# A 7 x 7 softmax-weighted convolution on one core: other slots of taps, 32-row tiles for the two small layers, logits computed twice

## The chip, the core and the metric

One core of one Trainium2 chip runs the whole program in one launch. The metric is the device time in microseconds (us) of that launch. Five engines work side by side, each through its own list in order, and wait for one another through semaphores: TensorE (PE, with its weight loads as PEld), VectorE (DVE), ScalarE (ACT), GpSimd (POOL) and SyncE (SP), which issues most DMAs.

## What is computed

The program has two layers. The second (attention and a feed-forward part on chosen tokens) is not touched and follows the first. The first is, on 4 images of 256 channels and 56 x 56 pixels, after a group normalization:

```
x1 = conv1x1(x, w1, b1)            # 32 channels
x2 = conv1x1(x, w2, b2)            # 32 channels
x3 = conv1x1(x, w3, b3)            # 256 channels
p  = conv1x1(position(h, w), wp, bp)   # 2 channels, the same for all images
sub2 = x1[:, :, None] - unfold_patches(x2)     # 49 taps, reflected borders
subp = p[:, :, None] - unfold_patches(p)
y = relu(bn_eval(concatenate([sub2, subp]), bn1))   # 34 channels
y = relu(bn_eval(conv1x1(y, cw1), bn2))             # 32 channels
wgt = softmax(conv1x1(y, cw2, cb2), axis=taps)      # 32 channels x 49 taps
out[:, l, s] = sum over taps of x3[tap][:, l, s] * wgt[:, l, tap]   # s: 8 channels share a weight
x = x + out
```

All is float32.

## The kernel before

`conv_layer` first makes *planes*: image by image, in strips of 8 rows (`planes(n, q)`, 7 strips an image), it normalizes x, makes x1, x2 and x3 and stores them in DRAM, x2 and x3 with their reflected borders (`x3d`), x1 in `a1d`. Strips of later images are made while earlier images are worked on.

The main work goes in *blocks* of 4 rows, 14 an image, 56 in all. The 49 taps of a block are packed into *slots*: one instruction on 128 partitions handles four taps (four groups of 32 channels), because a group reads its plane one column or one row further on. Here there are 13 slots (`SLOTS`), 10 with four taps and 3 with three (96 partitions). For column slots the planes sit in rings (`xc` for x3, `ac` for x2), for row slots in windows loaded anew for each block (`xw`, `aw`).

A block passes through three generators:

- `relation`: `differ` (POOL, x1 - x2 in four groups of slots), `bend` (ACT, relu), `hidden` (PE, layer cw1 with a block-diagonal 128 x 128 matrix, by pairs of slots), `bend_more` (ACT, slot by slot, since in the inside of the image the position term is one number per slot, held in `tb`), the six border columns apart (`borders`, `place_borders`, `bend_borders`), `logits` (PE, layer cw2), `keep` (ACT, to SBUF in `lg`).
- `softmax`: `begin`, `largest`, `split`, `join`, `turned`, `over_turned` (the maximum over slots and over the four groups, by a tree on DVE and two turns on PE), `lower` (DVE, subtract it), `exponents` (ACT), `add_up`, `gather`, `spread`, `invert` (the sum's reciprocal).
- `values`: for each slot a product of 8 planes with the slot's exponentials, 128 x 1792 elements, 8 slots on DVE (`OURS`, the weights copied to PSUM first by `weights`) and 5 on POOL (`POOLS`), and `add`, four matmuls with the matrix `same` that add the groups up in PSUM (`acc`); then `divide`, `more` (+ x) and `store`.

`by_quarters` splits a 128-column layer into four matmuls with 32 columns, which lie in four column parts of the array (the profile's "128*32": 128 rows, 32 columns). The trace shows two matmul records for each float32 matmul.

The order is written out by hand: `AT` gives for each step of a block its place in a round, in steps of a fourteenth of a round (`ROUND = 14`) and a rank. The loop at the end of `conv_layer` emits one round per block, with steps of three or four blocks mixed. `InOrder` keeps that order on each engine. `side` holds the planes, the statistics of the next image, and `ready`, the second layer's normalization of image 0, which advance one piece per step. SP issues the loads in the same order (`load_relation`, `load_first`, `load_values`).

Of the kernel before, what the change touches and what calls it, by code (L numbers as in the profile page):

```python
# [15 lines left out]
P = 128  # L16
NB = 4
# [41 lines left out]
def bn_affine(nc, pool, par, n, eps, tag):  # L59
# [15 lines left out]
    [(ki, 0, COLUMN, 4) for ki in range(KS)]  # L75
    + [(0, kj, ROW, 4) for kj in range(4, KS)]
    + [(ki, 4, COLUMN, 3) for ki in range(4, KS)]
)
NS = len(SLOTS)
ORDER = [0, 1, 2, 3, 4, 5, 6, 10, 11, 12, 7, 8, 9]  # L80
POOLS = [1, 3, 5, 7, 9]
OURS = [i for i in range(NS) if i not in POOLS]
GROUPS = [(0, 4), (4, 7), (7, 10), (10, 13)]
HALVES = [(0, 10), (10, 13)]
INNER = W - 2 * PAD
RB = 4
ROUND = 14
KEPT = 12
RING = KEPT + 3
QUADS = (H + 2 * PAD + 3) // 4  # L90
FB4 = RB * W


AT = {
    "load_relation": (-12, 4), "load_first": (23, 4), "load_values": (32, 5), "differ": (-5, 6),
    "bend": (-2, 9), "load_pos": (-1, 7), "hidden": (4, 5), "borders_0": (1, 5),
    "place_borders_0": (3, 9), "bend_borders_0": (6, 9), "borders_1": (3, 5),
    "place_borders_1": (7, 0), "bend_borders_1": (14, 3), "bend_more": (5, 5), "logits": (7, 1),
    "keep": (8, 7), "begin": (22, 1), "largest_0": (23, 3), "largest_1": (25, 6), "split": (27, 0),
    "join": (27, 7), "turned_0": (28, 7), "over_0": (29, 1), "turned_1": (29, 4), "over_1": (30, 1),  # L100
    "lower_0": (30, 1), "exp_0": (31, 0), "lower_1": (32, 5), "exp_1": (32, 8), "lower_2": (31, 9),
    "exp_2": (33, 0), "add_up_0": (33, 4), "add_up_1": (33, 5), "gather": (34, 1),
    "spread": (34, 1), "invert": (36, 1), "weights": (31, 5), "ours": (33, 0), "add_ours": (34, 0),
    "pools": (33, 6), "add_pools": (36, 9), "divide": (47, 1), "more": (51, 7), "store": (55, 3),
}
PLANE = WP * WP
NPL = SH + 1
# [3 lines left out]
def conv_layer(ctx: ExitStack, tc: tile.TileContext, d, xs: bass.AP, ln0: bass.AP):  # L111

# [7 lines left out]
    a1d = dram.tile([NB, REL, HW], F32, name="a1d")  # L126
    posd = dram.tile([8, NS, 3 * FB4], F32, name="posd")
    bordersd = dram.tile([8, NS, 3 * FB4], F32, name="bordersd")
    insided = dram.tile([8, NS], F32, name="insided")

# [6 lines left out]
    chunk = lambda q: slice(q * CH, (q + 1) * CH)  # L137

# [4 lines left out]
    for q in range(NCH):  # L143
        sy.dma_start(x0[:, :, chunk(q)], whole_image(x, 0)[:, :, chunk(q)])

    par = const.tile([P, len(COLS)], F32, name="par")
    nc.scalar.dma_start(par, d["par"])
    pposs = const.tile([8 * NS, 7], F32, name="pposs")
    nc.scalar.dma_start(pposs, d["par_pos"])
    gavg = const.tile([P, P], F32, name="gavg")  # L150
    nc.scalar.dma_start(gavg, d["gavg"])
    w12 = const.tile([P, 2, 2 * REL], F32, name="w12")
    nc.scalar.dma_start(w12, d["w12T"].rearrange("(c p) o -> p c o", p=P))
    w3 = const.tile([P, 2, C], F32, name="w3")
    nc.scalar.dma_start(w3, d["w3T"].rearrange("(c p) o -> p c o", p=P))
    cw1 = const.tile([P, P], F32, name="cw1")
    nc.scalar.dma_start(cw1, d["cw1_diag"])
    cw1p = const.tile([8, P], F32, name="cw1p")
    nc.scalar.dma_start(cw1p, d["cw1_pos"])
    cw2 = const.tile([P, P], F32, name="cw2")  # L160
    nc.scalar.dma_start(cw2, d["cw2_diag"])
    turn = const.tile([P, 2, P], F32, name="turn")
    nc.scalar.dma_start(turn, d["turn"])
    same = const.tile([P, P], F32, name="same")
    nc.scalar.dma_start(same, d["same"])
    eps = const.tile([P, 1], F32, name="eps")
    nc.vector.memset(eps, GN_EPS)

# [5 lines left out]


    sh12 = const.tile([P, 1], F32, name="sh12")
    nc.vector.tensor_scalar(sh12[:REL], s1[:REL], col("b1")[:REL], t1[:REL], ALU.mult, ALU.add)
    nc.vector.tensor_scalar(
        sh12[REL : 2 * REL], s1[REL : 2 * REL], col("b2")[REL : 2 * REL], None, ALU.mult
    )  # L180

    mm = ctx.enter_context(tc.tile_pool(name="mm", bufs=4, space=PSUM))
    xqp = ctx.enter_context(tc.tile_pool(name="xq", bufs=3))
# [3 lines left out]
    held = {}  # L187

    def load(n, q):

        t = xqp.tile([P, 2, CH], F32, tag="xq", name=f"xq{n}_{q}")
        sy.dma_start(t, whole_image(x, n)[:, :, chunk(q)])
        return t

    def statistics(n):

        st = sp.tile([P, 2, NCH, 6], F32, tag="st", name=f"st{n}")
        mv = sp.tile([P, 2, 2], F32, tag="mv", name=f"mv{n}")
        ts = held.pop(("xa", n))
        for q in range(NCH):  # L200
            for c in range(2):
                ve.bn_stats(st[:, c, q], ts[q][:, c])
            if len(ts) < NCH:
                ts.append(load(n, len(ts)))
            yield
        yield
        for c in range(2):
            ve.bn_aggr(mv[:, c], st[:, c].rearrange("p q s -> p (q s)"))
        pm = mm.tile([P, 512], F32, tag="mm", name=f"pm{n}")
        te.matmul(pm[:, 0:2], gavg, mv[:, :, 0], start=True, stop=True)  # L210
        yield
        gm = sp.tile([P, 2], F32, tag="gm", name=f"gm{n}")
        ve.tensor_copy(gm, pm[:, 0:2])
# [4 lines left out]
        pv = mm.tile([P, 512], F32, tag="mm", name=f"pv{n}")  # L218
        te.matmul(pv[:, 0:2], gavg, dv, start=True, stop=True)
        rs = sp.tile([P, 2], F32, tag="rs", name=f"rs{n}")  # L220
        se.activation(rs, pv[:, 0:2], AF.Sqrt, bias=eps)
# [10 lines left out]
    held["xa", 0] = [x0[:, :, chunk(q)] for q in range(NCH)]  # L232

    tb = const.tile([P, NS], F32, name="tb")
    near = const.tile([P, 3, NS * RB * 2 * PAD], F32, name="near")
# [5 lines left out]
    for j in range(2):  # L244
        nc.scalar.dma_start(loc[j * 4 * NS : (j + 1) * 4 * NS, :, 1], d["loc_from"])
    whole(statistics(0))

    def positions():

        pl = pp.tile([8 * NS, 2, 3 * FB4], F32, name="pl")  # L250
        ve.tensor_scalar(pl, loc[:, 0], pposs[:, 4:5], None, ALU.mult)
        yield
        ve.scalar_tensor_tensor(pl, loc[:, 1], pposs[:, 5:6], pl, ALU.mult, ALU.add)
        yield
        ve.tensor_scalar(pl, pl, pposs[:, 6:7], None, ALU.add)
        cen = pp.tile([8 * NS, 3 * FB4], F32, name="cen")
        ve.tensor_tensor(cen, pl[:, 0], pl[:, 1], ALU.subtract)
        yield
        se.activation(cen, cen, AF.Relu, bias=tp1, scale=sp1)
        inside = pp.tile([8 * NS, 1], F32, name="inside")  # L260
        ve.tensor_copy(inside, cen[:, FB4 + W // 2 : FB4 + W // 2 + 1])
        less = pp.tile([8 * NS, 3 * FB4], F32, name="less")
        ve.tensor_scalar(less, cen, inside, None, ALU.subtract)
        for j in range(2):
            r = slice(j * 4 * NS, (j + 1) * 4 * NS)
            nc.sync.dma_start(insided.rearrange("(g j) t -> j t g", j=2)[j], inside[r])
            nc.scalar.dma_start(bordersd.rearrange("(g j) t f -> j t g f", j=2)[j], cen[r])
            nc.sync.dma_start(posd.rearrange("(g j) t f -> j t g f", j=2)[j], less[r])
        at8 = pp.tile([8, NS], F32, name="at8")
        nc.sync.dma_start(at8, insided)  # L270
        edge = pp.tile([8, 3, NS, RB, 2, PAD], F32, name="edge")
        for b in range(3):
            for i in range(2):
                at = b * FB4 + i * (W - PAD)
                src = bordersd[:, :, at : at + 1]
                nc.scalar.dma_start(
                    edge[:, b, :, :, i],
                    bass.AP(
                        src.tensor, src.offset,
                        [list(src.ap[0]), list(src.ap[1]), [W, RB], [1, PAD]],  # L280
                    ),
                )
        for _ in range(10):
            yield
        pt = mm.tile([P, 512], F32, tag="mm", name="pinside")
        te.matmul(pt[:, :NS], cw1p, at8, start=True, stop=True)
        ve.tensor_scalar(tb, pt[:, :NS], s2, t2, ALU.mult, ALU.add)
        n = NS * RB * 2 * PAD
        for b in range(3):
            pt = mm.tile([P, 512], F32, tag="mm", name=f"pnear{b}")  # L290
            te.matmul(
                pt[:, :n], cw1p, edge[:, b].rearrange("p t h i w -> p (t h i w)"),
                start=True, stop=True,
            )
            ve.tensor_scalar(near[:, b], pt[:, :n], s2, t2, ALU.mult, ALU.add)

    second = slice(REL, 2 * REL)

    def planes(n, q):


        sh, rs = held["norm", n]
        f = slice(q * CH, (q + 1) * CH)
        at = f"{n}_{q}"
        t = held.pop(("xb", n, q))
        for c in range(2):
# [4 lines left out]
        issue = [sy, se] if n == 0 and q < 2 else [sy]  # L311
        yield
        pt = mm.tile([P, 512], F32, tag="mm", name=f"p12_{at}")
        for c in range(2):
            quartered(pt[: 2 * REL, :CH], w12[:, c], t[:, c], start=c == 0, stop=c == 1)
        yield
# [1499 lines left out]
```

## Time and profile before

| | us |
|---|---|
| median of 3 runs (lowest, highest) | 3694.44 (3693.19, 3697.65) |
| the profiled execution, and its span from first to last instruction | 3699.99, 3698.2 |
| span: until the first block's `divide` | 169.1 |
| first to last `divide` of the 56 blocks (55 steps) | 1631.6 |
| after the last `divide`: the second layer | 1897.5 |

The busy time of each engine between the first and the last `divide` is PE 1464.9, DVE 1497.2, ACT 1146.3, POOL 1412.3 of 1631.6 us; the DMA engines are busy 63% of it and move 135 GB/s. By image, taken from `divide` to `divide`:

| stretch of the span, us | length | PE | DVE | ACT | POOL | DMA |
|---|---|---|---|---|---|---|
| 169.1 to 581.4 | 412.3 | 376.3 | 376.9 | 304.5 | 340.6 | 65% |
| 581.4 to 1009.7 | 428.3 | 388.5 | 394.4 | 309.9 | 367.9 | 66% |
| 1009.7 to 1433.0 | 423.3 | 380.4 | 377.8 | 298.7 | 361.8 | 63% |
| 1433.0 to 1800.7 | 367.7 | 319.7 | 348.3 | 233.2 | 342.1 | 57% |

A `divide` is the DVE instruction `o<-acc,rz`; the time between two of them is the time of one block. Busy time of PE holds the pipelined ends of its matmuls, so a stream of n matmuls is best read from start to start. In a row of the groups, "out<-in" names the tiles (numbers left out) and the shape is partitions x elements.

### The profile page before, as it was taken

The page shows a single profiled execution, that of the slowest core. Times are in us where ns is not written, and L with a number is a line of the kernel's source. Part 1 is how long each engine was busy: PE and PEld are TensorE (multiplying, and loading weights), DVE is VectorE, ACT ScalarE, POOL GpSimd, SP SyncE. Part 2 cuts the span into 40 slices and gives each one's busy share as a digit, 9 for nine tenths or more (in the row PEclk, how much of TensorE's full clock was granted, in tenths as well). Part 3 has the DMA queues.
Part 4 walks back from the last instruction along what each step waited for, and adds up shares of the span by engine and source line. Part 5 has one row for each costly group of instructions (what it writes and reads, how often), then busy time and mean ns, then how long its engine had stood idle before and what let it go on. Part 6 is the DMA issues. An engine that isn't in the chain of part 4 may idle for free. (4 is left out here: it accounts for less than half of the span.)

```text
span 3698.2 us, 92932 instructions
## 1 busy us (share of the span) xinstructions
PE 3267.4 (88%) x38326; PEld 1431.4 (39%) x38326; DVE 2559.0 (69%) x3552; ACT 1941.0 (52%) x4104; POOL 1950.9 (53%) x1165
## 2 busy tenths in 40 slices
PE   3889997999879998899699979997899889989989
PEld 1334432443334333343243334333433344336666
DVE  2589989999889988999774567555864576534211
ACT  2768766787568766776235533453344424542111
POOL 1578887889778988998650035022602252211311
PEclk7999999999989999999899999999999999999999
DMA  3766657665666647655301210132013200231110
GB/s 101 159 149 149 148 134 164 150 139 109 153 146 150 129 97 147 124 120 109 102 2 45 65 49 7 37 96 61 8 32 80 62 18 13 64 93 47 55 49 26
DMA packets 328070, 332.00 MB, mean 90 GB/s; under 512 B 68651, under 2 KB 315407, under 8 KB 327647
## 3 DMA queue, kind: packets, MB, share of 16 engines
q1 hardware_dynamic: 309509, 289.68, 35.3%
q0 software_dynamic: 11408, 32.32, 2.7%
q8 instruction: 302, 4.95, 0.6%
q10 hardware_dynamic: 6730, 4.05, 0.5%
q14 instruction: 121, 0.99, 0.1%
HBM read 256.78 MB, written 68.68 MB: 88 GB/s over the span
## 5 line engine op out<-in xcount | busy, mean ns | idle before, releaser
L859 POOL TENSOR_TENSOR pr<-xc,lg 128x1792 f32<-128x1792 f32 x280 | 1039.4, 3726 | 220.1 <-DMA xc<-x3d 92.8
L859 PE MATMUL acc<-pr,same 128*32 128x448 f32 (+1 forms) x5824 | 718.5, 554 | 126.2 <-DVE pr L859 81.0
L859 PE MATMUL p<-y,cw 128*32 128x400 f32 (+5 forms) x6272 | 679.3, 511 | 3.0 <-ACT y L859 1.8
L859 ACT ACTIVATE ph<-pg,unit 128x896 f32<-128x896 f32 x448 | 426.7, 1004 | 474.7 <-PE pg L859 471.9
L859 DVE TENSOR_TENSOR pr<-xc,exp 128x1792 f32<-128x1792 f32 x280 | 559.6, 1999 | 41.0 <-DMA xc<-x3d 29.4
L859 POOL TENSOR_TENSOR phi<-ls 128x512 f32<-128x512 f32 (+1 forms) x200 | 246.2, 1231 | 348.3 <-PE accs L859 172.8
L859 ACT ACTIVATE y<-p,tb,bn2s 128x200 f32<-128x200 f32 (+1 forms) x728 | 341.7, 521 | 144.8 <-PE p L859 143.2
L859 PEld LDWEIGHTS acc<-pr,same 128*32 128x32 f32 (+1 forms) x5824 | 203.5, 111 | 432.4 <-DVE pr L859 181.5
L859 DVE TENSOR_TENSOR phi<-pv,ls 128x1408 f32<-128x1408 f32 (+1 forms) x200 | 322.0, 1619 | 64.7 <-PE accs L859 44.0
L859 PEld LDWEIGHTS p<-y,cw 128*32 128x32 f32 (+1 forms) x6272 | 236.2, 111 | 326.4 <-issue 216.3
L859 DVE TENSOR_TENSOR pr<-xw,exp 128x1792 f32<-128x1792 f32 x168 | 338.0, 2013 | 26.8 <-DMA xw<-x3d 14.5
L859 POOL TENSOR_TENSOR y<-a,ac 128x896 f32<-128x896 f32 x168 | 279.3, 1663 | 115.7 <-DMA ac<-x3d 87.2
L859 POOL DMA_DIRECT2D out<-tk x28 | 20.9, 747 | 543.0 <-ACT tk L859 532.3
L859 ACT ACTIVATE ls<-pv 128x256 f32<-128x256 f32 (+1 forms) x200 | 77.4, 387 | 389.5 <-PE pv L859 369.1
L859 PE MATMUL pg<-qT,pairs 32*128 32x448 f32 x1792 | 275.7, 593 | 6.2 <-ACT ph L859 4.1
L859 PE MATMUL pv<-wqkv,xn 128*32 128x256 f32 x3136 | 216.1, 391 | 49.0 <-DVE phi L859 29.7
L859 POOL DMA_INDIRECT us<-rows,to x112 | 109.6, 979 | 262.5 <-DMA us<-rows,to 231.8
L859 PE MATMUL accs<-phi,v 128*32 128x512 f32 (+1 forms) x1600 | 217.7, 608 | 26.3 <-DVE phi L859 25.7
L859 ACT ACTIVATE lg<-p,par 128x448 f32<-128x448 f32 x392 | 232.8, 594 | 2.5 <-PE p L859 2.4
L859 ACT ACTIVATE y<-y 128x896 f32<-128x896 f32 x224 | 180.7, 807 | 87.1 <-POOL y L859 87.0
L859 ACT ACTIVATE h<-ph,apar 128x512 f32<-128x512 f32 (+1 forms) x104 | 63.2, 658 | 293.3 <-PE ph L859 293.2
L859 PE MATMUL acc<-ph,cf 128*32 128x448 f32 (+1 forms) x1792 | 215.0, 551 | 0.0
(256 smaller groups left out, 5168.5 us busy)
## 6 DMA issues: line engine op xcount, KB each, us to landing
xw<-x3d SPq DMA_DIRECT2D x224, 248.0 KB
xq<-in_x SPq DMA_DIRECT2D x47, 448.0 KB
xc<-x3d SPq DMA_DIRECT2D x54, 248.0 KB
xc<-x3d SPq DMA_DIRECT2D x54, 247.0 KB
xc<-x3d SPq DMA_DIRECT2D x54, 246.0 KB
xc<-x3d SPq DMA_DIRECT2D x54, 245.0 KB
xr<-in_x SPq DMA_DIRECT2D x224, 56.0 KB
xs<-xr SPq DMA_DIRECT2D x224, 56.0 KB
```

The source lines that it names most:

```text
L859: return lambda *a, **k: self.tc.keep_in_program_order(of(*a, **k))
```

## The change

Everything is inside `conv_layer` and the arrays that the host lays out for it.

**Slots.** 12 slots of four taps, 48 taps round the centre; the centre tap is handled apart with the 4 rows of a block on the four groups of partitions (56 elements instead of 224; steps named `..._own`). Every slot has 128 partitions.

```diff
 SLOTS = (
-    [(ki, 0, COLUMN, 4) for ki in range(KS)]
-    + [(0, kj, ROW, 4) for kj in range(4, KS)]
-    + [(ki, 4, COLUMN, 3) for ki in range(4, KS)]
+    [(ki, 0, COLUMN) for ki in range(3)]
+    + [(ki, 3, COLUMN) for ki in range(4, KS)]
+    + [(0, kj, ROW) for kj in range(4, KS)]
+    + [(3, kj, ROW) for kj in range(3)]
 )
+PARTS = ((0, 8), (8, 12))
+POOLS = (2, 5, 8, 11)
+OURS = tuple(t for t in range(NS) if t not in POOLS)
```

**Layers on sixteen parts.** `hidden` and `logits` multiply 32 x 32 weights, with a row part r and a column part j for each matmul, into bank r of a PSUM tile `quad` of four banks, for 8 slots and then for 4. The position term becomes a second matmul of two rows for every block (`posm`, or `posb` in border blocks); the border steps and `tb`, `near` go. `bend_more` is one ACT instruction for 8 slots and one for 4.

```diff
+            for r in range(4):
+                for j in range(4):
+                    te.matmul(
+                        quad[group(j), r, : m * FB4], cw1[group(r)],
+                        view(y1[group(r)], (a + j) * FB4, [[4 * FB4, m], [1, FB4]]),
+                        start=True, stop=False, skip_group_check=True,
+                    )
+            for r in range(4):
+                two = slice(r * REL, r * REL + 2)
...
+                    te.matmul(
+                        quad[group(j), r, : m * FB4], cw1p[two], of,
+                        start=False, stop=True, skip_group_check=True,
+                    )
```

**Logits twice.** `logits` writes them to `quad` only for the maximum: one `tensor_reduce` on DVE over 8 slots (128 x 1792 in, 128 x 56 out) and one over 4. `keep`, `begin`, `split`, `join`, `turned`, `over_turned` and `lower` go. `lowered` makes the logits again in `quad` and takes the maximum off with further matmuls by `minus`; `exponents` reads `quad` and writes the weights `ws`.

```diff
+            ve.tensor_reduce(
+                held["mm", k][:, i], view(quad, 0, [[1, W], [512, 4], [W, 4 * m]]), AX.XY, ALU.max
+            )
...
+        def lowered(i):
...
+                    te.matmul(
+                        quad[group(j), r, : m * FB4], cw2[group(r)],
+                        view(y2[i][group(r)], j * m * FB4, [[1, m * FB4]]),
+                        start=True, stop=False, skip_group_check=True,
+                    )
...
+                    te.matmul(
+                        quad[group(j), r, : m * FB4], minus[group(r)],
+                        view(mxs[group(r)], 0, [[0, m], [1, FB4]]),
+                        start=False, stop=True, skip_group_check=True,
+                    )
```

`add_up` sums over slots into 128 x 56 (52 matmuls of 56 columns), `invert` takes 56 elements, and `spread` (16 matmuls of 56 columns and 128 rows) lays the maximum, the reciprocal and the centre's weight out over 224 elements.

**PSUM.** One tile `quad` (4 banks), one bank `small` for all small results, the planes, the statistics and `ready` (`bank()`), one bank `acc`, two for `exps`; each exists once.

**Loads.** `xw` becomes a ring of rows like `xc` (`rows_kept(..., ROW)`; one new quad of 4 rows a block, and 3 rows copied behind the ring's end each third block). New per block: `x3c` (the centre of x3), `aq` (centre of x1 and x2 by rows), 7 rows instead of 4 in `aw`. x1 is stored in `x3d` with borders; `a1d` goes. Position terms are stored once in `posd`, and the small loads of 12 bytes (`edge`) go.

**Planes.** A strip is made in named steps: x1 and x2 of both halves in one PSUM tile and one ACT instruction, x3 copied by ACT instead of DVE; a strip every second block, all the way.

**Places.** A new table `AT`, with `ROUND = 250`; all steps of all blocks, planes and side pieces are sorted by place and emitted in that order.

```diff
+    "load_relation": -120, "load_places": -94, "load_planes": -48, "differ_2": 0, "differ_3": 50,
...
+    "hidden_1": 116, "bend_0": 121, "bend_more_1": 126, "edges_both": 128,
+    "store_both": 136, "load_first": 148, "hidden_0": 151, "differ_own": 170, "bend_more_0": 173,
+    "bend_own": 200, "logits_0": 209, "load_second": 235, "hidden_own": 239, "bend_more_own": 244,
+    "largest_0": 246, "logits_own": 253, "logits_1": 259, "keep_own": 263, "largest_1": 272,
+    "values_0": 273, "most": 285, "keep_values_0": 285, "spread_most": 290, "load_own": 294,
+    "keep_most": 316, "lowered_0": 322, "values_1": 326, "lower_own": 337, "exp_0": 341,
...
+    "exp_own": 363, "exp_1": 364, "weights_1": 364, "product_1": 376, "edges_values": 376,
+    "product_2": 378, "store_values": 384, "weights_3": 385, "weights_4": 389, "add_up": 394,
...
+    "divide": 603, "more": 635, "store": 647,
...
+    for _, _, name, do, of in sorted(events, key=lambda e: e[:2]):
```

## The prediction

> **What bounds it now.** I read the busy time in windows first, with the block as unit (from one `divide` to the next). The blocks come in three kinds: a plain one of 25.7 us (most of image 3), one with a strip of planes 28.8, one with planes and `ready` 33.9. Four plain blocks, one with planes, one with both; columns are length, then PE, PEld, DVE, ACT, POOL, clock, DMA share, GB/s:
>
> ```profile
> core 0: us, PE busy (x) PEld busy (x) DVE busy (x) ACT busy (x) POOL busy (x), PEclk, DMA share, GB/s
> 1490.00:1592.90 102.90, 92.86 (x1128) 42.25 (x1124) 102.14 (x97) 75.03 (x160) 102.90 (x41) 1.00 0.59 120
> ...
> 1083.00:1112.00 29.00, 27.71 (x330) 12.83 (x328) 27.08 (x27) 23.07 (x56) 26.66 (x11) 1.00 0.69 157
> ...
> 641.00:675.00 34.00, 31.85 (x370) 14.35 (x362) 31.12 (x33) 27.46 (x65) 28.72 (x12) 1.00 0.70 156
> ```
>
> In plain blocks POOL never rests (102.90 of 102.90) and DVE hardly (102.14): POOL sets the end. With planes POOL has gaps and PE has none. The groups give the durations:
>
> ```profile
> L859 POOL TENSOR_TENSOR pr<-xc,lg 128x1792 f32<-128x1792 f32 x168 | 623.5, 3725 | 217.0 <-DMA xc<-x3d 92.8 <-ACT lg L859 76.4 <-PE acc L859 32.4
> ...
> L859 DVE TENSOR_TENSOR lg<-lg,z 128x1120 f32<-128x1120 f32 x112 | 147.1, 1313 | 1.9
> L859 DVE TENSOR_TENSOR z<-lg,z 128x448 f32<-128x448 f32 x224 | 139.7, 624 | 7.8 <-ACT z L859 3.9
> ...
> L859 ACT ACTIVATE lg<-p,par 128x448 f32<-128x448 f32 x336 | 208.2, 620 | 2.5 <-PE p L859 2.4
> ```
>
> The first row's idle time shows that xc's loads are waited for at the ends of images: blocks of 46.6, 53.0 and 36.4 us there.
>
> **POOL, before and after.** In its timeline a product starts 3.67 us after the last; `differ` takes 1.93 and 3 x 1.47, `more` 1.1. Before: 5 x 3.67 + 1.93 + 4.4 + 1.1 = 25.8, the plain block. After: 4 x 3.67 + 4 x 1.47 + 0.33 (`differ_own`; the 64-element POOL row takes 341 ns) + 1.1 = **22.0**.
>
> **DVE.** Products stay 8, at 1.94 start to start = 15.5. Gone: `lower` 2 x 1.31 + 0.84, the tree of maxima 3.5 + 1.15, `invert` 1.55, borders 0.74, and 1.4 per strip (x3's copy, now ACT's). New: two reductions, from this row, 1.18 ns an element:
>
> ```profile
> L859 DVE TENSOR_REDUCE w<-uw 112x4 f32<-112x1024 f32 x28 | 33.9, 1211 | 0.0
> ```
>
> so 2.1 + 1.05. That row reads SBUF in order; the new ones read four PSUM banks in steps of 56, which no row shows: not under 2.0 ([...]as in the products), at most perhaps twice, 6.3 for both; I take 3.15. `most` 0.3, `lower_own` 0.2, `invert` 0.45 (between the reciprocal rows 112 elements, 821 ns, and 224, 1554), `product_own` and `divide` 0.6 each. Sum 20.8, with the next image's statistics 21.4, against 25.6 before. VectorE: DVE Perf Modes, "Rules for kernel authors", speaks against this: the reduction is the slowest DVE operation, and one should restructure. By the row it costs 3.45 with `most` and replaces 4.65 of tree: it gains.
>
> **ACT.** A plain block had 18.8 busy. From 438 ns at 224 and 620 at 448 elements, 0.81 ns an element: 1792 take 1.71, 896 take 0.98. `bend` 1.7 + 0.9, `bend_more` and `exponents` 2 x 2.7, `weights` 2.8, small steps 1.9, planes 2: about 15. It lies beside PE and DVE.
>
> **PE: the step on which I rest.** A float32 matmul of 448 columns is two records; four column parts start 7 ns apart and the next pass 0.37 us later, so a group of four costs 0.75. Before: `hidden` 4.3, borders 0.5, `logits` 4.85, turns 0.75, sums 1.9, `add` 13 x 0.75 = 9.7: 22.0; with a strip (4.5) 26.4, and that block took 28.8: PE bound at **1.09 times** its sum. After, a round of sixteen matmuls of 448: 0.75 plus 16 x 7 ns of issue = 0.85, a second one on the same parts 0.75. `hidden` 1.6 + 0.85, `logits` 0.85 + 0.5, `lowered` 1.6 + 0.85: 6.2 (7.5 rounds at 448: 3, 1.5 and 3). `add` 13 x 0.75, `spread` 3 x 4 x 0.094, `add_up` 13 x 0.094, the centre 0.2: 18.5. Short matmuls run at their length here: the 65-column group (`accq<-ls`) starts every 36 to 56 ns per four.
>
> Against that stands a rule of TensorEngine Tiling (Array Packing), "Key Properties": a change of tiling mode drains the engine. The border block shows it, 128-row matmuls, then 8-row ones, and back:
>
> ```profile
> 86.74 0.99 PE L859 MATMUL p<-y,cw 128*32 128x400 f32 x8
> 87.66 0.91 PE L859 MATMUL p<-pos,cw1p 8*32 8x400 f32 x8
> 88.50 0.96 PE L859 MATMUL p<-xq,w 128*32 128x448 f32 x8
> ```
>
> Eight of 400 columns stream 0.68; the starts are 0.92 and 0.84 apart, so a switch costs 0.15 to 0.25. Six stages between 128-row work make 12 switches, 2.4 us. **Plain block 20.9, with a strip (3.75) 24.65.** Without the drain 18.5: then POOL binds.
>
> That all sixteen parts run at once is not in this trace. It shows four column parts, and four row parts by themselves:
>
> ```profile
> 2082.46 1.03 PE L859 MATMUL pg<-qT,pairs 32*128 32x448 f32 x8
> ```
>
> eight records of 448 in 1.03, as for columns. Ends: 0.75 a round (all at once) and 4 x 0.75 = 3.0 (only four at a time). I take the first end, since rows and columns each show no loss. TensorE: Matmul & The Clock Gate, "Measured speedup vs the span model", gives 10.6-fold for sixteen: 16 x 0.75 / 10.6 = 1.13 a round, 8.5 for the stages, +2.3 us a block, 3575 us in the end. I prefer the rows, because that figure holds one pack's start and tail.
>
> **The single `quad`.** Its users form a ring: `hidden_1`, `bend_more_1`, `hidden_0`, `bend_more_0`, `logits_0`, `largest_0`, `logits_1`, `largest_1`, `most`, `spread_most`, `keep_most`, `lowered_0`, `exp_0`, `lowered_1`, `exp_1`. PE 6.6, ACT 5.4 + 0.44, DVE 3.45, seven matmul tails of 0.17: 17.1, with 15 handovers of 0.05 17.9. Nearly 5 us a block are left for its steps to stand behind others: a reduction behind a product (1.94), `lowered_1` behind `add` and, in strips, `values_1` and `both` (3 us together). That cover hides the ring; beyond it each us a block is 55 us in all.
>
> **DMA and SP.** Per block: `xw`'s wrap 0.25 MB and its first quads 0.07, `x3c` 0.25, three more rows of `aw` 0.09, `aq` 0.06, and bordered x1: +0.75 MB on 4.0 (135 GB/s over 29.7 us). At 215 GB/s for full DMA engines (135 / 0.63) that is 22.1 us a block, hidden under 24.8 with a share of 0.87. SP issues about 39 DMAs a block at 0.46: 18 us, beside all this; `load_first` waits on SP for `product_2`, but what stands behind it is needed most of a block later. At an image's end the row ring has a spare quad, so I take 12 us lost a time where the mean excess of the three was 18.6.
>
> **The sum.** Plain block: PE 20.9 x 1.09 = 22.8 (POOL 22.0 just under). With a strip 24.65 x 1.09 = 26.9. Of 55 steps 26 have a strip: 26 x 26.9 + 29 x 22.8 = 1361. `ready`, 7 strips of four groups of 448: 7 x 3.3 = 23 (its DVE part, 4 us, has room now). Ends 36. First `divide`: before, 94 us from the first `differ` (75.0) for some 3.7 rounds of the table; now 603 of 250, 2.4 rounds of 24.8, in the same proportion some 53, so at about 130. 130 + 1361 + 23 + 36 = 1550, against 1800.7: -251. The second layer is the same. Profiled execution 3700.0 - 251 = 3449; the median of the runs is 5.6 lower: 3443, said as **3440**.
>
> **Rivals.**
>
> - *Everything hides, POOL alone binds* (0.12): 55 x 22.0 + 59 + 130 = 1399, **3293**. For it: POOL's sum was exactly the plain block. Against: PE, POOL, DVE and DMA then stand within 1.5 us of one another, in a fixed order.
> - *DMA or the ring binds* (0.28): no slice of the page's DMA row passes 0.8; 22.1 / 0.8 = 27.6 a block, 1518 + 36 + 130 = 1684, **3578**. The ring with 10 us of waits gives the same.
> - *Slower: sixteen parts do not run at once* (0.10). Place: the 7.5 rounds in `quad`; price at four at a time 22.4 for 6.2, so (22.7 + 16.2) x 1.09 = 42.4 a block and **4430**. It decides from a round of 1.39 us on (stages 10.4), fewer than 9 parts at once: then the mean block is back at 29.3.
> - The forecast has 0.50. That the change doesn't do what it says I can't find; all steps feed a result.
>
> **Range.** 3290 to 3600 holds the forecast, the DMA case, the page's 10.6 and the upper half of the first rival; it leaves out 0.10 on the slow side and some of the rest. Faster 0.87, within 0.2% (7 us, what a measurement can tell) 0.02, slower 0.11.
>
> **What would show it.** Right: PE's start-to-start of a stage of 448 in `quad` near 0.85 for 32 records; POOL products 4 a block at 3.7; `TENSOR_REDUCE` rows near 2.1 and 1.05; blocks near 23 and 27 alternating. Wrong: DMA share above 0.9 with `xc`, `xw` as releasers; ACT, DVE idle behind PE with `quad` long held; reductions of 4 us; a first `divide` later than 170.

## The result, and the profile after

The changed kernel takes 3877.28 us (median of 4 runs, 3869.75 to 3883.32) beside 3693.82 of the kernel before in the same session: ratio 1.0494, 95% interval 1.0472 to 1.0515. It is slower, where 3440 had been forecast. The profiled execution took 3874.12 us, its span 3871.6.

All of the loss is in the blocks. The first `divide` is at 164.1 us (169.1 before), the last at 1972.0 (1800.7), and the rest takes 1899.6 us (1897.5). The window between the two, with the columns length, PE, PEld, DVE, ACT, POOL (instructions), clock, DMA share, GB/s:

```profile
164.10:1972.00 1807.90, 1471.53 (x36252) 606.87 (x36252) 1228.22 (x925) 790.46 (x1396) 1209.37 (x548) 0.89 0.70 145
```

DVE, ACT and POOL work 269, 356 and 203 us less than before in this stretch, and PE as long; yet it is 176 us longer: 32.87 us a block in the mean, where it was 29.67. POOL and DVE fill 67% and 68% of it. The groups show that the durations are those the prediction took (columns: busy, mean ns of one, then idle time before them and its releaser; the row by itself is of before):

```profile
L911 POOL TENSOR_TENSOR pr<-xw,w 128x1792 f32<-128x1792 f32 x112 | 414.5, 3701 | 321.5 <-PE acc L911 151.4
L911 DVE TENSOR_TENSOR pr<-xw,exp 128x1792 f32<-128x1792 f32 x224 | 442.7, 2008 | 194.3 <-ACT exp L911 192.9
L911 PE MATMUL quad<-mxs,minus 32*32 32x224 f32 (+1 forms) x3584 | 142.7, 529 | 218.6 <-ACT mxs L911 218.3
```

```profile
L859 DVE TENSOR_TENSOR pr<-xc,exp 128x1792 f32<-128x1792 f32 x280 | 559.6, 1999 | 41.0 <-DMA xc<-x3d 29.4
```

What has grown is the idle time: ahead of all its products POOL stands idle for 567 us in place of 220, DVE for 293 in place of 68. The waits between the two `divide`s (us in total, times, longest) have no single head:

```profile
PEld acc L911 <- issue: 257.8, 750, 2.7
PEld small L911 <- issue: 246.9, 616, 4.5
ACT xb L911 <- DMA xb<-in_x: 243.2, 24, 18.5
DVE pr L911 <- ACT exp L911: 235.8, 72, 15.6
PEld quad L911 <- ACT mxs L911: 218.3, 22, 17.6
PE quad L911 <- ACT mxs L911: 200.7, 22, 16.8
POOL pr L911 <- ACT w L911: 195.9, 23, 16.3
ACT y L911 <- PE quad L911: 171.8, 65, 8.4
ACT exp L911 <- DVE pr L911: 162.4, 75, 7.2
```

The third line was priced at nothing in the prediction: a strip's load, for which ACT waits. The timelines of one block with a strip show what hangs on it; first SP's queue, then ACT, then PE (start, length, engine, operation; idle time before in brackets):

```profile
1637.77 6.32 SPq L911 DMA_DIRECT2D xc<-x3d  x4
1644.19 1.04 SPq L911 DMA_DIRECT2D xb<-in_x  x1
```

```profile
1643.33 0.36 ACT L911 ACTIVATE exp<-w 128x224 f32<-128x224 f32 x1 [2.09 <-DVE pr L911]
1651.27 1.41 ACT L911 ACTIVATE xb<-xb,sh,rs 128x448 f32<-128x448 f32 x2 [7.58 <-DMA xb<-in_x]
1652.59 0.42 ACT L911 ACTIVATE mxs<-small,par 128x224 f32<-128x224 f32 x1
```

```profile
1646.09 1.05 PE L911 MATMUL quad<-y,cw 32*32 32x448 f32 x32
1653.07 1.81 PE L911 MATMUL quad<-mxs,minus 32*32 32x448 f32 x32 [5.93 <-ACT mxs L911]
```

SP spends 6.3 us on `load_first`, and the strip's load stands behind it. ACT's `normal_0` stands idle for 7.6 us and starts 7 us after that issue, and `keep_most` is queued behind `normal_0`; `lowered_0` on PE waits for `keep_most` with `quad` half made, and everything after waits for `quad`. Two more things are to be seen in PE. Its matmuls of `lowered_0` take 1.81 us where the round of sixteen before took 1.05: the clock has fallen. And PE stops with nothing to wait for:

```profile
1631.63 0.24 PE L911 MATMUL small<-w,same 128*32 128x56 f32 x2 [1.32 <-issue]
...
1631.94 1.03 PE L911 MATMUL quad<-y,cw 32*32 32x448 f32 x32
1632.72 1.38 PE L911 MATMUL quad<-posm,cw1p 2*32 2x448 f32 x32
```

The first line is a hole of 1.32 us inside `add_up`. The other two start 0.78 apart: a round of sixteen parts, so they do run at once.

Three counts over the trace's records follow the runs below. *Idle of PE*: no record of PE or PEld, and the part of it in which the next instruction has no semaphore to wait for; 166 us and 0 before, 336 and 69 after. Of the 51 such holes over 0.3 us, 1.3 us long in the mean, 49 end between 1.2 and 1.6 us after a 16 KB transfer of the instruction queue has landed; by chance it would be 3. There are 284 of these transfers after, one for 255 records of PE, and 132 before. *Half clock*: time at a granted clock of 0.5, 96 us before, 403 after. *ACT's idle time at `normal_0`*: 300 us over 26 strips after, 243 of it over the 24 strips between the two `divide`s.

### The profile page after: what moved, and what is told of

Its sections match the earlier page's. It is cut to its first block, busy times and chain, and to the rows that moved or that the text cites. A ratio compares the mean times of both kernels' runs of the same rounds, so it can differ in the third digit from the quotient of the medians.

```text
span 3871.6 us, 130713 instructions
## 1 busy us (share of the span) xinstructions
PE 3247.0 (84%) x58144; PEld 1443.8 (37%) x58144; DVE 2271.2 (59%) x2994; ACT 1545.4 (40%) x2792; POOL 1735.5 (45%) x1165
## 5 line engine op out<-in xcount | busy, mean ns | idle before, releaser
L911 PE MATMUL acc<-pr,same 128*32 128x448 f32 x5376 | 649.9, 588 | 5.3 <-issue 4.3
L911 POOL TENSOR_TENSOR pr<-xw,w 128x1792 f32<-128x1792 f32 x112 | 414.5, 3701 | 321.5 <-PE acc L911 151.4
L911 DVE TENSOR_TENSOR pr<-xw,exp 128x1792 f32<-128x1792 f32 x224 | 442.7, 2008 | 194.3 <-ACT exp L911 192.9
L911 POOL TENSOR_TENSOR pr<-xc,w 128x1792 f32<-128x1792 f32 x112 | 415.0, 3705 | 245.4 <-ACT w L911 210.7
L911 PE MATMUL quad<-y,cw 32*32 32x224 f32 (+1 forms) x10752 | 319.5, 476 | 63.3 <-DVE mm L911 22.6
L911 PE MATMUL quad<-mxs,minus 32*32 32x224 f32 (+1 forms) x3584 | 142.7, 529 | 218.6 <-ACT mxs L911 218.3
L911 POOL DMA_DIRECT2D out<-tk x28 | 20.9, 747 | 545.0 <-ACT tk L911 534.4
L911 PEld LDWEIGHTS acc<-pr,same 128*32 128x32 f32 x5376 | 161.0, 117 | 264.9 <-issue 241.8
L911 ACT ACTIVATE y<-quad,bn2t,bn2s 128x896 f32<-128x896 f32 x112 | 164.4, 1468 | 182.2 <-PE quad L911 182.1
L911 ACT ACTIVATE exp<-w 128x224 f32<-128x224 f32 x448 | 154.9, 353 | 167.6 <-DVE pr L911 165.8
L911 ACT ACTIVATE w<-quad,par 128x1792 f32<-128x1792 f32 x112 | 154.6, 1380 | 160.6 <-PE quad L911 158.4
L911 POOL TENSOR_TENSOR y<-a,aw 128x672 f32<-128x672 f32 x112 | 167.1, 1515 | 89.8 <-DMA aw<-x3d 80.8
```

Source lines behind the costliest of these rows:

```text
L911: return lambda *a, **k: self.tc.keep_in_program_order(of(*a, **k))
```

## The experiments

Three causes are set against one another: the strip's load at the head of ACT's queue; PE's own supply and clock; the transfers. The expectations name them, in part by letters. "E1" and so on are the runs by the first part of their labels. Each ratio is to the kernel before in the same session (3688 us beside E1, E2, E3 and E13; 3684 beside E4, E6 and E7; 3685 beside E8 to E11; 3694 beside E12).

**E1, the strip's load early.**

```diff
-    "load_relation": -120, "load_places": -94, "load_planes": -48, "differ_2": 0, "differ_3": 50,
+    "load_relation": -120, "load_places": -94, "load_planes": -160, "differ_2": 0, "differ_3": 50,
```

> One edit: the place of load_planes in the table goes from -48 to -160, so that SP issues a strip's 448 KB of x some 11 us earlier, ahead of the loads of both rings. Nothing else changes. Theory A (ScalarE stands at normal_0 until the strip's x has landed, with keep_most and exp_0, links of the quad ring, queued behind it): the idle time before normal_0, 11.6 us a strip and 300 us in all in the changed kernel, falls below 3 us a strip; of it 150 to 260 us leave the time, which is then 3620 to 3730 us. Theory B (the DMA engines are full in these blocks, so that the bytes are late wherever they are issued): the strip lands in time, but the ring loads behind it come as much later, DVE and POOL wait for xc and xw, and the time falls by under 60 us, to 3820 or more. Theory C (PE's own supply of instructions and its half clock set the block): idle time before normal_0 falls, PE's waits grow by as much, 3830 or more.

3823.18 us, 1.0373 [1.0347, 1.0398]. ACT's idle time at `normal_0` is gone, all 300 us, but the time falls by 54 only (45 by the two ratios). In the profiled runs 13 us are gained before the first `divide` and 30 between the `divide`s; the second layer, which no edit touches, takes 1880 to 1910 us in them, so that whole times of single runs can differ by 30 us from that alone. The window and the waits of this run:

```profile
150.70:1928.00 1777.30, 1523.03 (x36252) 635.93 (x36248) 1229.51 (x924) 795.41 (x1395) 1210.87 (x548) 0.88 0.70 149
```

```profile
POOL pr L911 <- PE acc L911: 327.8, 45, 20.9
PEld small L911 <- issue: 324.5, 588, 10.0
ACT y L911 <- PE quad L911: 266.9, 60, 12.5
```

ACT's wait has become one of ACT and POOL for PE: `y` for `quad` 172 to 267, `pr` for `acc` 151 to 328. Idle of PE without a wait rises to 148 us, half clock to 440.

**E2, the strip's load at its old place but issued by ACT.**

```diff
-        sy.dma_start(t, whole_image(x, n)[:, :, chunk(q)])
+        (se if tag == "xb" else sy).dma_start(t, whole_image(x, n)[:, :, chunk(q)])
```

> The place of load_planes stays at -48, but the load is issued by ScalarE's queue instead of SP's. It tells why the load is late. If SP's order holds it back (it stands behind load_first, which waits for products, and its eight ring loads), it is issued at ScalarE's own pace, some 5 to 10 us sooner against normal_0, and the idle time before normal_0 falls by at least half: 3680 to 3780 us. If it is the bytes ahead of it in the DMA engines, issue to normal_0 grows as the issue moves ahead, and the time stays at 3840 to 3900.

3876.77 us (one run): no gain, though ACT's idle time at `normal_0` falls to 7 us or less. That is neither of the two expectations. With E1: the wait is real, and taking it away lays bare others of nearly the same length.

**E3 and E13, `spread` by the whole array**: 4 matmuls of 128 columns in place of 16 of 32, so 8 000 fewer instructions; E13 has E1's edit too.

```diff
-                    quartered(
+                    te.matmul(
```

> The three spreads of a block use four matmuls with all 128 columns of weights instead of sixteen with 32: 36 matmuls (72 records and as many weight loads) fewer a block of some 332, the sums the same. Theory C' (PE runs short of instructions: it is idle 69 us between the first and the last divide with no semaphore to wait for, before 0, mostly in add_up and the spreads, right at 16 KB instruction fetches): this idle time falls by a tenth to a half, 7 to 35 us, and the time by 10 to 60 us. If that idle time is something else, it and the time stay within 10 us, or the time grows by up to 30 us since a 128-column spread has [...]longer weight loads.

> The early strip load and the whole spreads together. If the two costs are apart, the gains add up: the time is that of the early load alone less 10 to 60 us. If the block is bound by something else once the strip's wait is gone (POOL 22.0 us a block, the quad ring), the second edit adds under 10 us.

3915.17 us, 1.0624 [1.0586, 1.0662], and 3893.94, 1.0568 [1.0539, 1.0596]: slower by 38 and 71 us than without the edit, by the medians. Idle without a wait falls (69 to 46 and 148 to 129), but the three spreads now keep PE busy for 202 us, where they took 129: a weight load of 128 columns takes 191 to 229 ns in the mean, one of 32 columns 110 to 126. Fewer instructions at the price of PE time don't pay here.

**E4, position matmuls over 32 rows**, 30 of them zero, with E1's edit: as many instructions, columns and results, more active rows.

```diff
+    nc.vector.memset(posm, 0.0)
...
-                two = slice(r * REL, r * REL + 2)
+                two = group(r)
```

> On top of the early strip load: the position matmuls read all 32 partitions of their group (30 of them zeros, weights and data) instead of 2. The same matmuls, columns, tiles and result; only the active rows differ. Theory D (the granted clock goes to half after a 3.4 us window in which the active rows x columns of the streaming matmuls fill less than about a third of the array: in the early-load run nine in ten of the onsets followed a window under 0.33, and of the windows without onset 98% lay above 0.35; a 2-row matmul fills a sixteenth of what a 32-row one does): the time at half clock, 440 us between first and last divide there, falls to 200 to 330 us, and the time by 30 to 120 us, to 3700 to 3795. If the onsets come from PE standing idle and not from narrow matmuls, half clock stays at 400 to 460 us and the time within 15 us.

3793.83 us, 1.0302 [1.0281, 1.0323], 29 less than E1, at the edge of what was expected (30 to 120). Half clock falls from 440 us to 290 with idle without a wait unchanged (152): rows that multiply zeros keep the clock up. PE's busy time falls by 64 us, and its waits for others grow by 30.

**E6, without the loads of the row ring** from the fourth block on, with E1's edit; the row slots multiply the first blocks' planes.

```diff
-        rows_kept(n, [b + 1], xw, slice(0, SH), ROW)
+        if k < 3:
+            rows_kept(n, [b + 1], xw, slice(0, SH), ROW)
```

> On top of the early strip load: the row ring of x3 is loaded for the first three blocks only and then read as it is (the row slots' planes are left out from then on, so the values are not the layer's). It takes 1.3 MB of some 4.8 MB a block off the DMA engines and no work off PE, DVE, ACT or POOL. Theory B (DMA engines): the time falls by 250 us or more, to the region of 25 us a block. Theory C (PE short of instructions because their 16 KB fetches queue among the data): PE's idle time without a wait, 148 us in the early-load run, falls below 60 us, and the time by 100 to 250 us. If the fetches are late by themselves, or the order and the single quad hold the block, the idle time stays above 100 us and the time falls by under 100 us.

3612.67 us (one run), 210 less than E1. The window:

```profile
151.60:1721.40 1569.80, 1417.80 (x36252) 600.13 (x36252) 1249.60 (x925) 793.85 (x1394) 1210.55 (x550) 0.94 0.56 124
```

PE, DVE, ACT and POOL have the same instructions, and from `divide` to `divide` 208 us are gone: 28.54 a block. Idle of PE without a wait falls from 148 to 49, half clock from 440 to 191. Theory C's two numbers came true; theory B's 25 us a block did not.

**E12, the same loads with one plane of eight**: as many issues, an eighth of the bytes.

```diff
-        rows_kept(n, [b + 1], xw, slice(0, SH), ROW)
+        rows_kept(n, [b + 1], xw, slice(0, SH if k < 3 else 1), ROW)
```

> The kernel after with E1's earlier load; from the fourth block on each load of the row ring is issued as before, with its waits and its place on SP, but brings one plane of eight (the row slots multiply planes of the first blocks in the other seven). It tells the bytes from the issues in E6's gain of 210 us. If the bytes cost (transfers slow each other and the instruction fetches): nearly all of E6's gain, 3600 to 3650, idle of PE without a wait about 50 us. If the issues cost (about four a block of 0.46 us and their waits on SP, which hold up the loads behind them): 3740 to 3820 as in E1, and E6's gain is SP's.

3705.04 us (10 runs, 3683 to 3716), 1.0012 [0.9997, 1.0028]. Idle without a wait is 68 us, half clock 273. The time falls between the two expectations: of E6's 210 us, 118 go with the bytes and 92 with the issues by the medians, 133 and 76 by the ratios to before. What an issue does beyond its bytes (its place on SP, its semaphores, the landing that a product waits for) was not taken apart.

**E7, the kernel before with twice the matmuls** (`hidden`, `logits` cut in four by columns), **E9, the kernel before with 0.75 MB more of DMA a block**, **E8, both.**

```diff
+                for i in range(2 * (e - t)):
+                    m = RB * INNER // 2
...
+        more = dram.tile([P, 6, RB, WP], F32, name=f"more_{k}")
+        rows_shifted(n, b, more, slice(0, 6), [sy])
```

> The kernel before, with the two small layers' matmuls cut in four by columns (100 or 112 columns in place of 400 or 448; hidden uncut in border blocks): some 300 matmuls a block instead of some 155, the same columns in all, the same tiles, results and waits. Theory C (instructions alone cost, by their supply): PE idles 40 to 150 us without a wait between first and last divide, where the kernel before had 0, and the time grows by 40 to 250 us. If PE's supply holds at this density, both stay: 0 to 10 us idle and a time within 0.5%.

> The kernel before with only the 0.75 MB more of DMA a block. Theory C: before has the cover, its DMA share goes from 0.63 to about 0.75 and the time by less than 1% (3690 to 3725), idle without a wait under 15 us. Rival (data arrive late once the share passes 0.7, whatever the instructions): over 3% slower, with xc and xw as releasers of POOL and DVE.

> The kernel before with its hidden and logits matmuls cut in four (E7: twice the matmul instructions, +0.6%) and 0.75 MB more of DMA a block, copies of planes of x3d into an unused place in DRAM; all results are as before. Theory C (instruction fetches stand among the data transfers): the two together cost more than each by itself: PE idle without a wait over 40 us between the first and the last divide (7.8 in E7), and the time over E9's by more than E7's 12 to 17 us, by 50 us or so: 3790 to 3850 in all. Rival (the loads cost by themselves, the instructions nothing): the time is E9's plus at most 20 us, idle without a wait stays under 15 us.

E7 3705.43, 1.0059 [1.0038, 1.0079]; E9 3734.05, 1.0136 [1.0119, 1.0153]; E8 3756.69, 1.0194 [1.0177, 1.0211]. E8 is E9 plus 23 us, E7 before plus 22: the two add up, and idle without a wait is only 18 us in E8 (8 in E7, 0 in E9), just over what the rival allowed. So at E8's density instruction fetches among many transfers cost little. E9 lies between its two expectations. E8's window shows how near it is to the changed kernel in both:

```profile
173.50:1857.40 1683.90, 1489.35 (x31766) 890.80 (x31758) 1498.36 (x1456) 1147.17 (x2584) 1411.78 (x544) 0.96 0.68 157
```

63 524 records of PE in 1684 us are 38 a microsecond; the changed kernel has 72 504 in 1808, 40. The transfers are 264 MB and 263. In the old order this costs 2%. The two are alike in the mean only: 3.2 us of E8 hold at most 232 instructions of PE (112 in before), of the changed kernel up to 384. So E8 is a test of the mean density and not of the bursts.

**E11, the kernel before without its row windows' loads** from the third block on, E6's counterpart.

```diff
+        if k < 2:
             xw = x3p.tile([P, SH, RB, WP], F32, tag="xw", name=f"xw_{k}")
...
+        else:
+            xw = held["xw", k % 2]
```

> The kernel before with its row windows loaded for the first two blocks only (later blocks' row slots multiply those planes, so the output differs). Control for E6. Theory C: before is held by POOL and PE, so the time falls by less than 1.5% (3640 to 3690) though 1 MB of 4 a block goes. Rival (loads are late in both kernels alike, and E6's 210 us have nothing to do with the change): it falls by 100 us or more, to under 3590.

3665.73 us, 0.9950 [0.9933, 0.9967]: 19 us for 55 MB less. E6 took away 70 MB and gained 210.

**E10, E4's and E6's edits together.**

> The kernel after with E1's earlier load, E4's 32-row position matmuls and E6's left-out loads of the row ring (the row slots read planes of the first blocks from the fourth block on, so the row slots' products are of other planes). Theory C with the clock: both effects add, mean block near 27.9 to 28.1, time 3570 to 3590, half clock about 100 us, idle without a wait under 50. Rival (clock and fetches only hide a wait in the order of the steps): no gain over E6, 28.5 a block and 3612. The forecast's 24.8 a block is reached in neither; what is left is then the order and the single quad.

3603.27 us, 0.9769 [0.9750, 0.9787].

```profile
150.80:1715.60 1564.80, 1398.33 (x36252) 592.08 (x36252) 1260.47 (x924) 794.04 (x1396) 1211.20 (x548) 0.96 0.56 125
```

28.45 a block, 0.09 under E6, whose single time lies inside E10's runs (3594 to 3614); half clock 137 us for 191. With the transfers relieved, E4's edit brings little or nothing that these runs can tell.

**The ring, counted.** The records that touch `quad`, in order, give the time that its stages take and the time that it stands between them, in us a block:

| `quad` stands between | after | E1 | E10 |
|---|---|---|---|
| first matmuls of `lowered` and those by `minus` | 3.7 | 0 | 0 |
| `bend_more` and the next matmuls | 2.9 | 4.6 | 2.1 |
| a reduction and the next matmuls | 2.7 | 2.6 | 2.6 |
| `exp_0`, `exp_1` and the next matmuls | 2.2 | 2.3 | 2.2 |
| matmuls and a reduction | 1.7 | 1.6 | 1.7 |
| matmuls and ACT | 0.9 | 1.1 | 1.2 |
| elsewhere | 0.3 | 1.1 | 0.3 |
| all gaps | 14.3 | 13.2 | 10.1 |
| the stages themselves (block less gaps) | 18.6 | 19.1 | 18.4 |

In 8.8 us of the changed kernel's 14.3 the engine that comes next is at work on another step (6.8 PE, 1.5 DVE, 0.5 ACT); in 3.7 PE stands for `keep_most`. The handing over itself takes little.

**PE, counted.** The same stretch from the first to the last `divide`, in us, by what PE does (busy is matmuls and weight loads; half clock lies within the other columns):

| | whole | PE busy | idle, waits for others | idle without a wait | half clock |
|---|---|---|---|---|---|
| before | 1631.6 | 1466 | 166 | 0 | 96 |
| after | 1807.9 | 1472 | 267 | 69 | 403 |
| E1 | 1777.6 | 1524 | 105 | 148 | 440 |
| E4 | 1747.5 | 1461 | 135 | 152 | 290 |
| E12 | 1655.3 | 1455 | 132 | 68 | 273 |
| E6 | 1569.7 | 1419 | 102 | 49 | 191 |
| E10 | 1564.8 | 1399 | 111 | 55 | 137 |

From E1 to E6 PE's waits for others stay (105 and 102). The 208 us that hang on the row ring's loads are 105 of busy time, for the same instructions (half clock falls by 249, worth at most half of that), and 100 of holes without a wait. So in this kernel these loads cost through PE's clock and its supply of instructions, not through data that reach PE late. Which of the two starts it is not shown: a hole also empties the array, and the clock fell after one in the block above. In the old order E9's loads add 34 us of waits and no holes.

## Why the prediction was wrong

**The step that failed** is the price of a block, "PE 20.9 x 1.09 = 22.8" and "24.65 x 1.09 = 26.9", with what let it stand: "That cover hides the ring; beyond it each us a block is 55 us in all". The ring's own time was forecast at 17.9 us and is 18.6. Its gaps were left at nearly 5 us in a plain block and, in the forecast's mean block of 25.8 us (1420 / 55, with `ready` and the ends of images), at 7.9. They are 14.3. That is 6.4 of the 7.1 us by which the mean block is too long. The sum took the longest engine times 1.09 for the block; in the trace a chain of fifteen steps over one tile fills it, and its stages stand behind other work for 8.8 us of these gaps, most of it on PE itself. PE's sum of 22.7 us in the mean (20.9 and 24.65) would have needed a factor of 1.45, in E10 still 1.25.

The same 388 us, counted by PE: the forecast gave it 1270 us of work (26 x 24.65 + 29 x 20.9 + 23) and 150 for all the rest (9%, and the ends). Measured are 1472 of busy time, 69 without a wait and 267 of waits for others. Busy time holds some 5% more than such a sum (27.71 for 26.4 in the prediction's block with a strip, so PE was not quite without gaps there, 27.71 of 29.00). By that estimate some 140 of the 388 us are PE at half clock, which both the sum and the 1.09 left out, 69 are its holes without a wait and 180 are waits beyond what the 9% and the ends allowed. The two counts describe one loss in two ways; neither is a cause by itself.

What stands behind it, by the runs:

- *"It lies beside PE and DVE" (ACT's 15 us) and "what stands behind it is needed most of a block later" (SP).* Both wrong at one place. ACT's busy time is 12.4 to 15.8 us a block by image, but `normal_0` stood on ACT for its data ahead of `keep_most`. E1 shows the worth of it, some 50 us, while `quad`'s first gap shrinks by 3.7 us a block (201 us): PE waits 162 us less, but is busy 52 us and idle without a wait 80 us longer. As the main cause this wait is refuted.
- *DMA "hidden under 24.8".* The sizes were right (0.77 MB more a block for 0.75; 145 GB/s at a share of 0.70, so 209 at full share, for 215). That they are hidden was wrong: E6 shows 210 us that hang on the row ring's loads alone, at a mean share of 0.70, and E12 that over half of it goes with their bytes. The old order pays 19 us for such loads (E11) and 49 us for 42 MB more (E9).
- *"Short matmuls run at their length here."* Undisturbed, yes: a `spread` starts its 32 records in 0.38 us, as forecast (4 x 0.094). But the new rounds come in bursts. `add_up` and a `spread` are 136 matmul records with as many weight loads, 272 instructions, in some 1.6 us by the prediction's own lengths (17 x 0.094). A 16 KB transfer of the instruction queue brings some 255 by the count above, takes 0.9 to 1.4 us, is followed by work some 1.4 us after it has landed where PE stands still, and no two start less than 3.2 us apart in this trace: at most some 80 instructions a us, where the burst asks for 170. The Trainium skill (Runtime: NRT & Kernel Launch, "Instruction fetch mechanics") calls the crossing of such a 16 KB boundary mostly hidden. Before agrees (0 us of idle without a wait), the changed kernel does not: 69 us, 148 in E1. E8, with nearly the same mean density but at most 232 in 3.2 us, has 18 us.
- *The clock*, which the sum took at its full value. Half clock costs at most half its time: 202 us after, 48 before. E4 shows 29 us of the kernel's time to hang on it by itself; in E6 the clock rose with the transfers relieved, and no edit of rows.

**What was right**: POOL 22.0 us a block (22.0 in the mean, 20.8 to 22.7 by image), DVE 20.8 and 21.4 (22.3 in the mean, 20.9 to 23.5), the reductions 2.1 and 1.05:

```profile
L911 DVE TENSOR_REDUCE mm<-quad 128x56 f32<-128x1792 f32 x112 | 173.5, 1549 | 31.8 <-PE quad L911 25.5 <-PE small L911 5.7
```

1549 ns is the mean of 2.02 and 1.08, so reading four PSUM banks in steps costs no more than the row from SBUF, and no more than a product of as many elements (2008 ns). A round of sixteen at 0.78 (0.85 forecast) settles the rival "sixteen parts do not run at once" against it: the change is slower, but not by that mechanism. It is 15.4 times one matmul's rate (16 x 0.75 / 0.78), and this measurement decides against the 10.6-fold that the prediction set beside it. The switches of tiling mode (2.4 us) could not be told apart from other waits. The first `divide` came at 164, not 130; E1 shows 13 us of that to be the strip's load. Two slips in the prediction's sums change nothing: 22.1 / 24.8 is a share of 0.89, not 0.87, and 42.4 us a block come to about 4415 us, not 4430.

**The rivals.** The nearest is "DMA or the ring binds", with 10 us of waits in the ring and 3578 us. The changed kernel has 14.3: the term was too small by 4 us a block, and in the forecast itself by more. It should have been the rival on the slow side. E10 has just these waits (10.1 us) and takes 3603, but without the row ring's loads, so that this agreement is no test. Its DMA half, a bound at a share of 0.8, did not come about (0.70). No rival had the clock or PE's supply in it.

**What stays open.** That the single `quad` makes the kernel this sensitive is argued from the counted gaps and from E8, E9 and E11, which show the old order nearly unmoved by the same loads. The old order also lacks the bursts and the rounds of two rows, so by the count of PE these may be the reason as well. No run tells the two apart by freeing the ring: `quad` holds four of eight banks, `exps` two, `small` and `acc` one each, so a second `quad` has no room, and a smaller one was not tried. E10's mean block is still 2.6 us over the forecast; over half of that lies in the first 22 steps (31.4 us each, 26.5 in the rest), among them those with `ready`. No version that computes everything beat the kernel before; the best is E4 at 3794 us.

## What to carry to other kernels

When the sums of four engines come within a few us of one another and one buffer passes between them all, price the chain over that buffer with its queueing, not the longest engine alone: each handover stands behind whatever its engine has in hand, here about one us for each of fifteen, and time taken off one engine comes back in part as waits (E4: 64 us off PE's busy time, 30 of them back). Price PE at the clock that its matmuls will get, and look at the densest burst of short instructions, not at the mean. In an engine's queue look at the instruction that waits for data, and at who stands behind it, before calling that engine idle cover. And after taking one wait out, count what the others became: 300 us of one wait were worth some 50.

## What the hardware showed that was not expected

**The clock can fall while PE is busy.** The granted clock takes the values 0.5 and 1.0 and changes in steps of 3.41 us. The Trainium skill (TensorE: Matmul & The Clock Gate, "What's actually happening") gives such a window and has the gate follow how busy PE has been. The trace says what counts as busy. In half of the 58 steps ahead of a fall (changed kernel) PE had matmuls in less than 0.25 of the time, but in one of ten in over 0.7. With each matmul weighted by its active rows and columns, the array was at most a third full in 90% of them, and in 98% of the others it was fuller. In E1 the best line on the weighted share puts 2 of 390 steps on the wrong side, the best on the plain share 21. The block above shows a fall, at 1633.93:

```profile
1629.00:1631.90 2.90, 1.58 (x105) 1.40 (x104) 1.04 (x1) 2.23 (x6) 2.90 (x3) 1.00 0.27 47
1631.90:1634.80 2.90, 2.90 (x105) 1.58 (x103) 2.38 (x2) 0.66 (x1) 1.36 (x1) 0.85 0.35 79
1634.80:1638.00 3.20, 3.20 (x60) 1.19 (x48) 2.00 (x2) 1.60 (x3) 0.05 (x1) 0.60 0.43 67
...
1652.00:1656.00 4.00, 2.93 (x40) 0.69 (x44) 2.15 (x2) 3.08 (x6) 0.00 (x0) 0.50 0.92 191
```

In the 3.41 us ahead of it PE had matmuls for two thirds of the time, but weighted the array was 0.27 full: the hole of 1.32 us and a round of two rows lie in them. At half clock a group of four matmuls of 448 columns takes 1.49 us, not 0.75. E4's zero rows are the test: 150 us less of half clock.

**PE stands still where bursts of short matmuls follow one another, and starts again with the next transfer of instructions**, 1.3 us at a time after, 2.2 in E1, 1.1 in E6: 69, 148 and 49 us in all, none before. That it waits for its own instructions is read from the times at which the holes end; no run changed the supply alone.
